# Moving one ternary weight piece within a sequence's fusion, and the FFN norm's layout to the last recurrence pass

## The chip, the cores and the metric

The kernel runs on one core of one Trainium2 chip. The metric is the device time of one execution in microseconds; the median of three runs before the change is 1723.41 us (1723.16 to 1723.78). All times in the trace are counted from the start of the profiled span.

## The reference

Eight sequences of 512 tokens and 512 channels go through a four-layer bidirectional gated recurrence, a fusion of both directions, and a feed-forward network with ternary weights. Both directions use the same recurrence weights. Cut to what matters:

```python
def _mingru(x, Wz, bz, Wh, bh):
    z = sigmoid(x @ Wz.T + bz)
    h_tilde = tanh(x @ Wh.T + bh)
    a = clip(1.0 - z, 1e-8, 1.0 - 1e-8)
    return linear_scan(a, z * h_tilde)
def _stack(x, ...):                     # forward, and on the flipped sequence
    for i in range(4):
        h_new = _mingru(h, ...)
        if i > 0:
            h_new = h_new + h
        h = layernorm(h_new, gamma, beta)
x = x + concat(h_fwd, h_bwd) @ fusion_W.T + fusion_b
# feed-forward
Wq = sign(W) * min(round(abs(W) / (mean(abs(W)) + 1e-6)), 1)
h = gelu(layernorm(x) @ Wq_fc.T)
h = layernorm(h) * ln_w + ln_b
x = x + h @ Wq_proj.T
```

## The kernel before

The channels lie on the 128 partitions in four chunks (`NC_` = 4), the tokens in four tiles (`NT` = 4). A sequence index is `b`; a recurrence stream is `s = (b, direction)`. The sequences are taken in pairs: (0, 1), (2, 3), (4, 5) and (6, 7). For each pair, layers 1 to 3 run over the streams (b,0), (b,1), (b+1,0), (b+1,1); then the two sequences are fused, tile by tile, with the first layer of the next pair put between the fusion tiles. The feed-forward network (FFN) runs after all eight sequences.

All the order is written out by hand. Each engine executes its instructions in the order in which the program issues them. One **slot** (`slot`, L407) issues a piece of main work on the tensor engine (PE), then the due turns and turns back of layer norms, then the scans, then the end of the main work.

- A **gates** slot (L422) does one output chunk of a layer: four matmuls by the program, eight in the trace, into a PSUM tile `u`; three activations on ScalarE (ACT: `a`, `t`, `z`, L444 to L446); on VectorE (DVE) a clip (L450), a product (L451) and a scan (L455). In the last layer the residual sums (L520) follow.
- A **turn** (L301) transposes one token tile into a PSUM tile `pt`. DVE takes its statistics (L156, L158, L162, L167), GpSimd (POOL) the inverse root (L163), ACT the normalised tile `tok` (L173, L174). There are two `pt` buffers (`ps_t`). A **turn back** (L310) transposes four `tok` tiles into `pf`, of which there are two buffers (`ps_f`).
- A **fusion tile** (`tile_of`, L536) adds the bias to a row tile on DVE (L542), takes a number of weight pieces (L543), does sixteen matmuls (L548) into two PSUM tiles, and at its end adds them to the row (L558) and stores it (L561).
- A **first-layer** chunk (L470) is scaled on DVE (L477) and scanned in both directions.

**Weight pieces.** The list `extra` holds small independent jobs; `pieces(n)` (L398) takes n of them and issues the loads of up to three pieces from the head of the list ahead. First come 32 pieces that sum absolute weights, then the thresholds; then 32 pieces that make the weights ternary (`quantised`, L599): two DVE operations (L178, L179) from a loaded tile (`fcb` or `pwb`, three buffers in `stgp`) into a tile `q` (two buffers in `qp`, named `fcq` and `pwq` in the trace), and a store to DRAM (L605) on SP's DMA queue. The tuple in L543 sets how many each fusion tile takes: four in the fusion of an even sequence, eight in that of an odd one. The four of sequence 0 are the end of the sums and thresholds; the ternary pieces run from sequence 1 to sequence 5, when they are used up.

**The norm's layout.** In the last pair, `combined()` (L616) adds four more jobs to `extra`: they spread the FFN norm's weight and bias over a tile `comb`, each as a rounded part (L623) and a remainder (L624). They are taken one after each gates slot of one stream's last layer (L524). `comb` is read first in the FFN, at L768. In the same passes the FFN's input of sequence 0 is turned: PE transposes into `py` (L199, in the `pf` buffers), ACT writes `yhi` (L204), DVE `ylo` (L205).

Of the kernel before, what the change touches and what calls it, by code (L numbers as in the profile page):

```python
# [24 lines left out]
def kernel(  # L25
# [27 lines left out]
    B, S, H = x.shape  # L53
    L = gru_wT.shape[0]
    F = fc_wT.shape[1]
    NC_ = H // P
    NT = S // P
# [61 lines left out]
    for i in range(2):  # L119
        s = const.tile([P, P], F32, name=f"fpick{i}")  # L120
# [88 lines left out]
    NW = NQ * NC_  # L209
# [4 lines left out]
    with rec:  # L214
# [58 lines left out]
        def need(*keys):  # L273

            while any(left.get(k) for k in keys):
                slot(None, 2)
# [48 lines left out]
        def norm(s, zs, tag, pause, pair=1):  # L325

            toks, at = Tokens(), now[0] + pause

            def dst():
                if s not in state:  # L330
                    state[s] = hp.tile([P, NC_, S], F32, tag="h", name=f"h_{s[0]}{s[1]}")
                return state[s]

            for t in range(NT):
                queue(turns, s, at, t // pair, tokens(turned(zs, t, f"{tag}_{t}", NC_), toks, None, f"{tag}_{t}"))
            for c in range(NC_):
                queue(backs, s, toks, c // pair, back(toks, dst, c, True, f"{tag}_{c}"))

        def norm_last(s, tag):
            rsv[s] = small.tile([P, NT], F32, tag="rsv", name=f"rsv_{tag}")  # L340
            zs = [state[s][:, c, :] for c in range(NC_)]
            for t in range(NT):
                queue(turns, s, now[0] + NC_ + 1, t, tokens(turned(zs, t, f"{tag}_{t}"), None, rsv[s][:, t : t + 1], f"{tag}_{t}"))
# [45 lines left out]
        extra = []  # L389
# [8 lines left out]
        def pieces(n):  # L398

            for _ in range(min(n, len(extra))):  # L400
                for piece in extra[:3]:
                    if piece[0] is not None:
                        piece[0]()
                        piece[0] = None
                extra.pop(0)[1]()

        def slot(work=None, cap=1, long=False):  # L407

            end = work() if work is not None else None
            due("factors")  # L410
            if long:
                due("scans")
            last = shares(cap) + x_shares()
            due("scans")
            if end is not None:
                end()
            due("resid")
            for f in last:
                f()
            now[0] += 1  # L420

        def gates(h, l, o, name, scans):  # L422

            def work():
                u = ps_u.tile([P, S], F32, tag="u", name=f"u_{name}")
                for c in range(NC_):
                    nc.tensor.matmul(  # L427
                        u, lhsT=gw[l][:, c, ts(o, P)], rhs=h[:, c, :],
                        start=(c == 0), stop=(c == NC_ - 1),
                    )  # L430
                z = zp.tile([P, S], F32, tag="z", name=f"z_{name}")
                zlive[0] += 1
                a, t = factors(u, z, l, o, name)

                def end():
                    product(a, z, t)
                    scans(a, z)
                return end
            return work
# [13 lines left out]
        def scan(dst, a, z, backward):  # L453
            d = slice(None, None, -1) if backward else slice(None)
            nc.vector.tensor_tensor_scan(dst[:, d], a[:, d], z[:, d], 0.0, ALU.mult, ALU.add)  # L455
# [47 lines left out]
        def layer(s, l):  # L503
            while s not in state:
                slot(None, 2)
            need(s)
            zs = []
            h = state[s]
            for o in range(NC_):
                def scans(a, z, o=o):  # L510
                    scan(z, a, z, s[1] == 1)
                    zs.append(z)
                    if l < L - 1:
                        nc.vector.tensor_tensor(z, z, h[:, o, :], ALU.add)  # L514
                    elif o == NC_ - 1:

                        for c in range(NC_):
                            def sums(c=c):
                                zlive[0] -= 1
                                nc.vector.tensor_tensor(h[:, c, :], zs[c], h[:, c, :], ALU.add)  # L520
                            stages.append((now[0] + c, "resid", sums))
                slot(gates(h, l, o, f"{s[0]}{s[1]}_{l}_{o}", scans))

                if s[0] < 2 and (l == L - 1 or o % 2) and len(extra) > 2 * NW or s == (B - 2, 1) and l == L - 1:  # L524
                    pieces(1)
            now[0] -= 1
            if l < L - 1:
                norm(s, zs, f"{s[0]}{s[1]}_{l}", 2)
            else:
                norm_last(s, f"{s[0]}{s[1]}_{l}")  # L530
            now[0] += 1

        def fusion(b):
            hs, rs = [], []

            def tile_of(t):  # L536
                def work():
                    if t == 0:
                        hs.extend(state.pop((b, d)) for d in range(2))
                        rs.extend(rsv.pop((b, d)) for d in range(2))  # L540
                    row = xs["f", b, t]
                    nc.vector.tensor_tensor(row, row, fb, ALU.add)  # L542
                    pieces((1, 2, 1, 0, 2, 2, 2, 2)[t + (b % 2) * NT])  # L543
                    pus = []
                    for d in range(2):
                        pu = ps_u.tile([P, H], F32, tag="u", name=f"pu_{b}_{t}_{d}")
                        for c in range(NC_):
                            nc.tensor.matmul(  # L548
                                pu, lhsT=hs[d][:, c, ts(t, P)], rhs=fw[:, d * NC_ + c, :],
                                start=(c == 0), stop=(c == NC_ - 1),  # L550
                            )
                        pus.append(pu)

                    def end():

                        assert all(left[b, d] < NT - t for d in range(2))
                        for d in range(2):
                            nc.vector.scalar_tensor_tensor(  # L558
                                row, pus[d], rs[d][:, t : t + 1], row, ALU.mult, ALU.add
                            )  # L560
                        nc.sync.dma_start(out=x1[b][t], in_=row)  # L561
                    return end
                return work
            return [tile_of(t) for t in range(NT)]
# [118 lines left out]
        for b in range(0, B, 2):  # L683
# [11 lines left out]
            for l in range(1, L):  # L695
                if last_pair:
                    load_fc(l - 1)
                    if l == 1:
                        combined()
                        load_pw(0)  # L700
                for s in ((b, 0), (b, 1), (b + 1, 0), (b + 1, 1)):
                    if l == L - 1 and not last_pair and s[1] == 0:
                        norm_x(s[0] + 2, now[0])
                    if l == L - 1 and s[1] == 0:
                        load_pair("f", s[0])
                    if l == L - 2 and not last_pair and s[1] == 1:
                        load_pair("n", s[0] + 2)
                        load_xT(s[0] + 2)
                    if last_pair and s == (b, 1) and l == L - 2:
                        load_y(0)  # L710
                    if last_pair and s == (b, 0) and l == L - 1:
                        norm_y(0)
                    layer(s, l)
                    if b == 0 and l == 1 and s[0] == 0:
                        fold_sums(s[1])
                    if b == 0 and l == 2:
                        if s[0] == 0:
                            fold(s[1])
                        elif s[1] == 0:
                            fold_bias()  # L720
# [34 lines left out]
    for i in range(2):  # L755
        s = const.tile([P, P], F32, name=f"pick{i}")
# [132 lines left out]
    for j in range(ends):  # L889
        b, k = divmod(j, NF)  # L890
# [81 lines left out]
```

## Time and profile before

| | |
|---|---|
| runs before, median of 3 | 1723.41 us (1723.16 to 1723.78) |
| profiled execution | 1722.93 us, its span 1720.9 us |
| granted PE clock | 0.999 |
| recurrence and fusion | 0 to about 1225 us |
| FFN | about 1225 us to the end |
| first fusion tile of an odd sequence starts at (PE, L548) | 321.18, 620.87, 919.90 us |
| last fusion tile of an odd sequence starts at (PE, L548) | 354.86, 654.56, 953.59 us |
| last layer of (6,1) on PE (L427) | 1117.35 to 1133.15 us |
| last layer of (7,1) on PE (L427) | 1151.93 to 1167.14 us |

The first column of a timeline line is the start in us, the second how long the group was busy; then engine, line, operation, tiles written and read, and the number of instructions; in brackets the idle time of the engine just before and what ended it. The ends of matmuls are modelled, so starts are compared with starts.

### The profile page before, as it was taken

The numbers are of one execution on the slowest core, as the hardware profiler recorded it, in microseconds if no ns is written. First come the engines' busy times: TensorE is split into PE (matmuls) and PEld (weight loads), VectorE is DVE, ScalarE is ACT, GpSimd is POOL, SyncE is SP. The second block draws the span as 40 slices with busy tenths as digits, with TensorE's granted clock in tenths as the row PEclk, the third lists the DMA queues.
The fourth block names the chain that finished last, engine by engine and source line by source line (L and its number), as shares of the span: only waits on it lengthen the run. The fifth ranks groups of instructions, "written<-read, shape, count | busy, mean of one in ns | idle before, by whom it ended". The sixth has DMA issues, their size and how long they took to land.

```text
span 1720.9 us, 19726 instructions
## 1 busy us (share of the span) xinstructions
PE 1703.8 (99%) x6424; PEld 1039.2 (60%) x6424; DVE 1452.0 (84%) x2865; ACT 1067.6 (62%) x1836; POOL 214.3 (12%) x334
## 2 busy tenths in 40 slices
PE   8999999999999999999999999999999999999998
PEld 4455554455555445555544555554688888888887
DVE  8989989889998998999899899995568778768876
ACT  4898883468886245888624688861266566566654
POOL 2111111111111111111111111110000000000000
PEclk9999999999999999999999999999999999999999
DMA  7002221250000115000012201202201101101100
GB/s 269 19 25 80 98 86 43 68 189 1 1 13 19 55 68 189 1 1 16 16 55 80 92 5 46 74 1 97 75 1 50 49 1 49 50 12 38 50 19 31
DMA packets 46454, 91.73 MB, mean 53 GB/s; under 512 B 5264, under 2 KB 5264, under 8 KB 45328
## 3 DMA queue, kind: packets, MB, share of 16 engines
q1 hardware_dynamic: 45488, 88.91, 15.0%
q10 hardware_dynamic: 864, 1.57, 0.3%
q8 instruction: 50, 0.82, 0.2%
q14 instruction: 52, 0.43, 0.1%
HBM read 65.30 MB, written 25.17 MB: 53 GB/s over the span
## 4 chain that ended last, share of the span: by engine, by line
PE 75%; DVE 19%; issue 4%; ACT 1%; POOL 0%; DMA 0%; DVEq 0%; POOLq 0%
PE u L427 29%; PE ph L789 12%; PE po L816 12%; PE pu L548 9%; PE pt L301 5%; DVE z L455 4%; PE pf L310 4%; PE u L470 3%; DVE st L156 3%; DVE z L451 2%; DVE zf L455 1%; DVE a L450 1%; DVE mv L158 1%; PE py L199 1%; DVE z L514 1%
## 5 line engine op out<-in xcount | busy, mean ns | idle before, releaser
L427 PE MATMUL u<-h,gw 128*128 128x512 f32 x768 | 345.5, 592 | 0.0
L427 PE MATMUL u<-xT,gw 128*128 128x512 f32 x768 | 345.4, 593 | 0.0
L455 DVE TENSOR_TENSOR_SCAN z<-a,z 128x512 f32<-128x512 f32 x224 | 274.2, 1224 | 7.6
L793 ACT ACTIVATE g<-ph 128x512 f32<-128x512 f32 x128 | 76.5, 597 | 240.5 <-PE ph L789 240.5
L427 PEld LDWEIGHTS u<-h,gw 128*128 128x128 f32 x768 | 138.7, 190 | 139.2 <-issue 138.7
L427 PEld LDWEIGHTS u<-xT,gw 128*128 128x128 f32 x768 | 138.7, 190 | 139.2 <-issue 138.0
L444 ACT ACTIVATE a<-u,ngb 128x512 f32<-128x512 f32 x192 | 131.7, 686 | 142.8 <-PE u L427 142.3
L156 DVE BATCH_NORM_STATS2 st<-pt 128x6 f32<-128x512 f32 x256 | 177.1, 692 | 49.7 <-PE pt L301 49.2
L163 POOL TENSOR_TENSOR rs<-ve,mhalf 128x1 f32<-128x1 f32 x192 | 123.0, 641 | 713.3 <-DVE nmu L167 658.3
L816 PE MATMUL po<-pwq,ghi 128*128 128x512 f32 x512 | 203.5, 397 | 0.0
L789 PE MATMUL ph<-yhi,fcq 128*128 128x512 f32 x512 | 199.7, 390 | 0.0
L816 PE MATMUL po<-pwq,glo 128*128 128x512 f32 x512 | 199.6, 390 | 0.0
L789 PE MATMUL ph<-ylo,fcq 128*128 128x512 f32 x512 | 199.4, 389 | 0.0
L451 DVE TENSOR_TENSOR z<-z,t 128x512 f32<-128x512 f32 x224 | 153.4, 685 | 8.5 <-ACT z L446 8.3
L174 ACT ACTIVATE tok<-pt,nmr,rs 128x512 f32<-128x512 f32 x192 | 149.3, 778 | 6.4
L804 DVE TENSOR_TENSOR acc<-acc,g 128x512 f32<-128x512 f32 x112 | 77.3, 690 | 87.9 <-ACT g L793 87.0
L446 ACT ACTIVATE z<-u,gb 128x512 f32<-128x512 f32 x192 | 132.4, 689 | 0.0
L445 ACT ACTIVATE t<-u,gb 128x512 f32<-128x512 f32 x192 | 130.8, 681 | 0.0
L301 PEld LDWEIGHTS pt<-ident,z 128*128 128x128 f32 x640 | 78.4, 141 | 82.4 <-issue 47.5
L548 PE MATMUL pu<-fw,xT 128*128 128x512 f32 x256 | 115.2, 593 | 0.0
L548 PE MATMUL pu<-fw,h 128*128 128x512 f32 x256 | 115.1, 592 | 0.0
L470 PE MATMUL u<-xT,gw 128*128 128x512 f32 x256 | 114.6, 593 | 0.3 <-DVE gw L673 0.3
(138 smaller groups left out, 2549.5 us busy)
## 6 DMA issues: line engine op xcount, KB each, us to landing
xn<-in_x_dram SPq DMA_DIRECT2D x32, 256.0 KB, 4.4
xf<-in_x_dram SPq DMA_DIRECT2D x32, 256.0 KB, 5.6
x<-xf SPq DMA_DIRECT2D x32, 256.0 KB, 2.0
xy<-x SPq DMA_DIRECT2D x32, 256.0 KB, 4.5
out_dram<-xy SPq DMA_DIRECT2D x32, 256.0 KB, 2.0
xT<-in_xt_dram SPq DMA_DIRECT2D x7, 1024.0 KB, 8.1
fca<-in_fc_wT_dram SPq DMA_DIRECT2D x16, 256.0 KB, 2.9
pwa<-in_proj_wT_dram SPq DMA_DIRECT2D x16, 256.0 KB, 2.6
```

Of the source, the lines that this page charges most:

```text
L156: nc.vector.bn_stats(st, src)
L174: nc.scalar.activation(dst, src, AF.Identity, bias=nmr, scale=rs)
L301: nc.tensor.transpose(pt[:, ts(c, P)], zs[c][:, ts(t, P)], ident)
L427: nc.tensor.matmul(u, lhsT=gw[l][:, c, ts(o, P)], rhs=h[:, c, :], start=(c == 0), stop=(c == NC_ - 1),)
L444: nc.scalar.activation(a, u, AF.Sigmoid, bias=ngb[:, l, o : o + 1], scale=-1.0)
L446: nc.scalar.activation(z, u, AF.Sigmoid, bias=gb[:, l, o : o + 1])
L451: nc.vector.tensor_tensor(z, z, t, ALU.mult)
L455: nc.vector.tensor_tensor_scan(dst[:, d], a[:, d], z[:, d], 0.0, ALU.mult, ALU.add)
L470: nc.tensor.matmul(u, lhsT=gw[0][:, c, ts(o, P)], rhs=xT[b][:, c, :], start=(c == 0), stop=(c == NC_ - 1),)
L548: nc.tensor.matmul(pu, lhsT=hs[d][:, c, ts(t, P)], rhs=fw[:, d * NC_ + c, :], start=(c == 0), stop=(c == NC_ - 1),)
L789: nc.tensor.matmul(ph, lhsT=w, rhs=ys[b][c][i], start=(c == 0 and i == 0), stop=(c == NC_ - 1 and i == 1),)
L816: nc.tensor.matmul(po[b][t], lhsT=part[:, ts(t, P)], rhs=pwq[k // NP_][:, k % NP_, :], start=(k == 0 and i == 0), stop=(k == NF - 1 and i ...
```

## The change

Two lines. The tuple in the fusion says how many pieces each tile takes: the first four numbers are for an even sequence, the last four for an odd one. For an odd sequence 2, 2, 2, 2 becomes 1, 2, 2, 3. The condition in `layer` now takes the four jobs of the norm's layout in the last layer of stream (7,1) instead of (6,1).

```diff
-                if s[0] < 2 and (l == L - 1 or o % 2) and len(extra) > 2 * NW or s == (B - 2, 1) and l == L - 1:
+                if s[0] < 2 and (l == L - 1 or o % 2) and len(extra) > 2 * NW or s == (B - 1, 1) and l == L - 1:
                     pieces(1)
...
-                    pieces((1, 2, 1, 0, 2, 2, 2, 2)[t + (b % 2) * NT])
+                    pieces((1, 2, 1, 0, 1, 2, 2, 3)[t + (b % 2) * NT])
```

Sequence 7 is odd too, but no piece is left when its fusion runs. In sequences 1, 3 and 5 the fifth to eighth number decide. The pieces keep their order; one piece of work in each of the three moves from the first tile to the last, after which the next pair's layer 1 begins.

## The prediction

> **What bounds the kernel now.** I read the page first (busy shares, the chain that ended last), then PE's waits, the windows by stage, and the timelines of PE, DVE, ACT and SP around the edited places.
>
> ```profile
> PE 1703.8 (99%) x6424; PEld 1039.2 (60%) x6424; DVE 1452.0 (84%) x2865; ACT 1067.6 (62%) x1836; POOL 214.3 (12%) x334
> ...
> PE 75%; DVE 19%; issue 4%; ACT 1%; POOL 0%; DMA 0%; DVEq 0%; POOLq 0%
> ...
> PE pt L301 <- ACT tok L174: 4.4, 11, 0.6
> ...
> 310.00:334.60 24.60, 24.07 (x79) 11.83 (x78) 23.51 (x47) 10.12 (x18) 3.15 (x5) 1.00 0.19 60
> 334.60:363.00 28.40, 28.40 (x98) 14.81 (x97) 22.02 (x40) 11.36 (x19) 2.05 (x3) 1.00 0.43 133
> ```
>
> PE is never idle for long; a change pays only where it closes a PE gap. The chain runs 19% through DVE, but most of that is DVE keeping pace. In the windows (length, then PE, PEld, DVE, ACT, POOL busy), 310 to 334.6 has DVE at 23.51 of 24.60 us while PE loses 0.5; the next has PE full and DVE with 6.4 us to spare. The gap between the two, on PE and on DVE:
>
> ```profile
> 328.92 3.60 PE L470 MATMUL u<-xT,gw 128*128 128x512 f32 x8
> 332.56 0.66 PE L301 MATMUL pt<-ident,z 128*128 128x128 f32 x4
> 333.70 0.66 PE L301 MATMUL pt<-ident,z 128*128 128x128 f32 x4 [0.49 <-ACT tok L174]
> 334.20 0.60 PE L310 MATMUL pf<-ident,tok 128*128 128x128 f32 x4
> 334.63 3.60 PE L548 MATMUL pu<-fw,xT 128*128 128x512 f32 x8
> ...
> 323.70 0.48 DVE L178 TENSOR_SCALAR fcq<-fcb,lo_fc 128x512 f32<-128x512 f32 x1
> 324.22 0.75 DVE L179 SCALAR_TENSOR_TENSOR fcq<-fcb,hi_fc,fcq 128x512 f32<-128x512 f32 x1
> 324.88 0.48 DVE L178 TENSOR_SCALAR fcq<-fcb,lo_fc 128x512 f32<-128x512 f32 x1
> ...
> 329.53 0.67 DVE L156 BATCH_NORM_STATS2 st<-pt 128x6 f32<-128x512 f32 x1
> ...
> 362.37 0.70 DVE L156 BATCH_NORM_STATS2 st<-pt 128x6 f32<-128x512 f32 x1 [4.34 <-PE pt L301]
> ```
>
> A chunk of eight matmuls holds PE 3.44 us start to start, four transposes 0.44. From 328.92 the two turns (L301), the turn back (L310) and the fusion matmuls could start at 332.36, 332.80, 333.23 and 333.67; the fusion starts at 334.63, so 0.96 us is lost. It is lost on DVE: the turns wait for a PSUM buffer that ACT's tok empties, tok waits for the statistics, and they stand behind the two weight pieces at 323.70 and 324.88. The stage recurs 298 us apart (PE turns at 633.40 and 932.43, equally late).
>
> The last pair has its own gap:
>
> ```profile
> 1132.99 0.60 PE L310 MATMUL pf<-ident,tok 128*128 128x128 f32 x4
> 1134.20 0.66 PE L199 MATMUL py<-ident,tok_y 128*128 128x128 f32 x4 [0.61 <-DVE ylo L205]
> ...
> 1130.08 0.68 DVE L624 TENSOR_TENSOR comb<-lnw,comb 128x512 fp32r<-128x512 f32 x1
> 1131.02 0.68 DVE L451 TENSOR_TENSOR z<-z,t 128x512 f32<-128x512 f32 x1
> 1133.46 0.68 DVE L205 TENSOR_TENSOR ylo<-py,yhi 128x512 fp32r<-128x512 f32 x1
> ...
> 1174.92 0.70 DVE L156 BATCH_NORM_STATS2 st<-pt 128x6 f32<-128x512 f32 x1 [2.73 <-PE pt L301]
> ```
>
> py is due at 1133.43 and starts at 1134.20: 0.77 lost, behind ylo, which stands behind two of the comb operations. Another 0.15 is lost at 1128.97.
>
> **What the Trainium skill says.** "Perfetto Trace Analysis", Optimization Strategy: look for the gaps of the engine that should be saturated and what they wait for; the trace bears it out, those gaps are the only place where this change can pay. "PSUM — Partial Sum Buffer", Engine vs sequencer instructions: VectorE's queue is strictly first in, first out, so whatever is behind a held ternary waits too; DVE's timeline keeps program order. "VectorE: DVE Perf Modes", TRN2 errata, gives 691 ns for a two-tensor f32 operation of 512 elements; L451 measures 685. "DMA: Bandwidth & Descriptors", Latency and other measured facts, has about 2 us of fixed cost per DMA; the stores of pieces (L605) land here 2.0 to 4.3 us after issue.
>
> **The change, part by part.** No instruction is added or removed overall: 32 weight pieces and four comb operations stay.
>
> *First tile of sequences 1, 3, 5: one piece fewer.* On SP a load and a store move later too. On DVE the pitch of a piece is 324.88 - 323.70 = 1.18 us. DVE has been without idle time since 309.55, so what follows moves up by 1.18 until something else holds it. That is the statistics at 329.53: they would reach 328.35, but read the turn that PE starts at 328.05, and statistics begin 0.64 after their turn (361.73 to 362.37, 366.48 to 367.12). So 328.69, a gain of 0.84. The second set, released afresh, follows 1.15 later (362.37 to 363.52), at 329.84 instead of 330.65: 0.81. POOL's and ACT's steps follow alike, tok from 332.87 to 332.06, and the second turn, 0.83 behind tok, from 333.70 to 332.89, where PE arrives at 332.80. Gain 0.81 of the 0.96. The other two stages have the same pitches (629.23 against a turn at 627.74; 928.25 against 926.77): 3 x 0.81 = 2.43 us. Does the wait come back? DVE later idles 0.92 before the scaling at 346.45, held by PE, so it catches up. The 0.39 that PE loses at 375.49 hangs on a chain restarted by PE at 366.48; it stays. So do the gaps before the edited tile (0.15 at 320.68, 0.59 at 620.38, 0.24 at 919.41).
>
> *Last tile: one piece more.* 1.18 us into 4.34 us of DVE idle before 362.37 (4.35 in the other two). The third ternary has a wait that the second has not: there are two q buffers (qp), so it needs the store of the tile's first piece landed. That store is issued at 356.87 and lands 3.14 later, 360.01; 0.81 earlier in the new order, 359.2. The third piece then ends at about 360.5, before the statistics' new 361.56: 1.1 us to spare. Its own load (issued 355.46, landed 359.31) comes sooner. For sequence 3 the store lands at 659.96, leaving 0.8 us; for sequence 5 at 957.61, over 2 us. Cost 0. Behind the waiting ternary stand the statistics of two turns and the x1 sums; an overrun would first use the 1.1 us by which tok (364.60, done 365.38) precedes PE's turn at 366.48. Bounds: 0 while the store lands within 5.3 us, one for one beyond (rival 3).
>
> *Comb operations out of sequence 6.* Ahead of ylo at 1133.46 go 0.34 (cast at 1125.52) and 0.60 (L624). Not all 0.94 counts: L451 at 1131.02 needs ACT's z, and follows z's start by 0.72 (1134.35 to 1135.07). ACT's three activations start 3.64 after PE's chunk (1129.55 to 1133.19); for the chunk at 1125.10 that is 1128.74 instead of 1128.80, so z starts at 1129.88 and L451 at 1130.60: gain 0.42. ylo and py follow, py 1133.78. Bounds: 0.3 (a 0.21 issue gap as at 1127.30 moving in front) to 0.92.
>
> *Comb operations into sequence 7's last pass.* DVE there runs at 3.87 us per slot (statistics at 1156.02, 1159.89, 1163.76), exactly PE's 3.44 + 0.43, without slack; so delays of 0.34, 0.94, 1.27 and 1.87 pile up. PE asks little of DVE there: a turn needs the buffer of two turns before, nearly 7 us earlier, and its h sums were finished by 1152.2, before the first added operation. The pile ends with the row addition at 1171.51, done at 1172.19 + 1.87 = 1174.06, before the 2.73 us idle ends at 1174.92. Cost 0; up to 1.87 without that cover. The comb's readers (L768) are in the FFN.
>
> **Sum:** -2.43 - 0.42 = -2.85 us. The profiled execution took 1722.93 (span 1720.9 and 2.0 around it), 0.48 below the median; the difference applies to either. 1723.41 - 2.85 = 1720.6.
>
> **The rivals.** A difference of 0.2% (3.45 us), about what can be told from no change, is the line between classes.
> (1) All of the gaps close: 3 x 0.96 + 0.77 + 0.15 = 3.80 us, 1719.6. For it: DVE and ACT have 0.2 us issue gaps near these places (335.23, 1127.30) that may move away. Against: the 0.64 behind the turn is measured twice, alike.
> (2) The gain is mostly taken back, say half: 1722.0, or 1723.4 if all. It would show as a new tok wait after 334.6. Against: DVE's 0.92 and 6.4 us of slack there.
> (3) Slower: the store wait. If, with its loads around it, the first store of the last tile took 7.5 us to land, the third piece would start at 363.5 and end at 364.8, 3.2 past 361.56; less the 1.1 before PE's turn, 2.1 per stage, 6.4 in three, and 6.4 - 2.85 = +3.6: 1727.0. A landing of 5.3 us begins to cost (3.14 + 1.1 + 1.1), and from 6.3 on the gain is gone. For it: a load took 1.57 us to issue at 655.15. Against: no piece store took over 4.3 us.
> That a piece simply doesn't move is excluded by the count: each odd sequence still takes eight, and four comb items remain for the last pass.
>
> **How the numbers follow.** Forecast (gain 2.2 to 3.45) 0.62; rival 1, 0.20; rival 2, 0.10; rival 3, 0.08. Faster by over 0.2%: 0.22 (rival 1 and the forecast's edge); within: 0.70; slower: 0.08. The range 1719.5 to 1722.3 holds the forecast, nearly all of rival 1 and half of rival 2.
>
> **What would show it.** Right: PE's fusion matmuls of the first odd tile 0.8 us sooner in three stages, the tok wait before them gone or 0.1; DVE idle in the last tile down from 4.34 to 1 to 2 us with the statistics still released by PE; py's wait on ylo near 0.35 instead of 0.77; DVE's 2.73 idle near 1174 down to about 0.9. Wrong: a third ternary waiting past 361, a PE wait between 1152 and 1175, or a tok wait that reappears after 334.6.

## The result and the profile after

The changed kernel takes 1720.88 us (median of 22 runs, 1720.01 to 1721.71), the kernel before 1723.59 (22 runs beside it): a ratio of 0.9984, 95% interval 0.9978 to 0.9990. The difference of 2.71 us is 0.16%, inside the 0.2% that the prediction takes as the line to no change, although the interval leaves out 1. The profiled span went from 1720.9 to 1718.0 us.

Because the profiled executions differ by up to 1.8 us before the first odd fusion tile (the turn ahead of its fusion matmuls starts between 320.57 and 322.33 us in the profiles below), the traces are compared over a **stretch**: from that turn to the second matmul of the FFN (PE, L789). It was 1226.09 - 320.68 = 905.41 us before and is 1223.19 - 320.57 = 902.62 after, 2.79 less.

From the page of the kernel after, the busy shares and the chain that ended last:

```profile
PE 1702.4 (99%) x6424; PEld 1039.2 (60%) x6424; DVE 1452.8 (85%) x2865; ACT 1067.8 (62%) x1836; POOL 214.6 (12%) x334
...
PE 79%; DVE 14%; issue 4%; ACT 1%; DMA 1%; POOL 0%; DVEq 0%; POOLq 0%; ACTq 0%
```

The work is the same. In the chain DVE's part fell from 19 to 14% and PE's rose from 75 to 79%. This says that DVE sets the pace less often, but not how much was gained: 5% of the span is 86 us, and the gain is 2.8. The waits and the windows show that. PE's waits after (total us, times, longest), then its windows around the first odd tile (length; PE, PEld, DVE, ACT and POOL busy; clock, DMA share, GB/s):

```profile
PE pt L301 <- ACT tok L174: 2.9, 8, 0.6
...
PE py L199 <- DVE ylo L205: 0.4, 1, 0.4
```

```profile
310.00:334.60 24.60, 24.60 (x82) 12.36 (x81) 23.13 (x48) 10.88 (x19) 3.39 (x6) 1.00 0.15 47
334.60:363.00 28.40, 28.40 (x98) 14.81 (x97) 23.26 (x43) 11.29 (x18) 2.04 (x4) 1.00 0.45 145
```

Three of the eleven listed waits for tok are gone, 1.5 us, and PE is full in the first window. DVE's 1.2 us went over to the second, from 22.02 to 23.26; the first falls by 0.38 only, since later work moves up into it. The first odd tile on PE's timeline after, and on DVE's:

```profile
328.81 3.60 PE L470 MATMUL u<-xT,gw 128*128 128x512 f32 x8
332.24 1.19 PE L301 MATMUL pt<-ident,z 128*128 128x128 f32 x8
333.27 0.60 PE L310 MATMUL pf<-ident,tok 128*128 128x128 f32 x4
```

```profile
324.10 0.75 DVE L179 SCALAR_TENSOR_TENSOR fcq<-fcb,hi_fc,fcq 128x512 f32<-128x512 f32 x1
324.77 0.42 DVE L450 TENSOR_SCALAR a<-a 128x512 f32<-128x512 f32 x1
...
328.57 0.70 DVE L156 BATCH_NORM_STATS2 st<-pt 128x6 f32<-128x512 f32 x1 [0.26 <-PE pt L301]
```

The clip L450 now follows one weight piece. The statistics are released by their turn (327.93, so 0.64 after it), no longer by DVE's queue, and the two turns on PE stand in one group. From its start to the turn back 1.03 us pass, where two turns without a wait take 0.87: about 0.15 of the 0.96 is left, as forecast. The fusion matmuls follow at 333.71 instead of 334.63: of this 0.92, 0.11 is the earlier chunk (328.81 against 328.92), 0.81 the gain.

The last tile on DVE's timeline after:

```profile
356.35 0.75 DVE L179 SCALAR_TENSOR_TENSOR fcq<-fcb,hi_fc,fcq 128x512 f32<-128x512 f32 x1
358.95 0.48 DVE L178 TENSOR_SCALAR fcq<-fcb,lo_fc 128x512 f32<-128x512 f32 x1 [1.85 <-DMA wq_fc<-fcq]
359.47 0.75 DVE L179 SCALAR_TENSOR_TENSOR fcq<-fcb,hi_fc,fcq 128x512 f32<-128x512 f32 x1
361.44 0.70 DVE L156 BATCH_NORM_STATS2 st<-pt 128x6 f32<-128x512 f32 x1 [1.23 <-PE pt L301]
```

The third piece waits 1.85 us for the store of the first (`wq_fc<-fcq`), ends 1.2 us ahead of the statistics, and PE still releases those. Of 4.34 us of idle time, 1.85 + 1.23 are left. The same place in sequence 3 is the closest of the three:

```profile
658.56 0.49 DVE L178 TENSOR_SCALAR pwq<-pwb,lo_pw 128x512 f32<-128x512 f32 x1 [2.55 <-DMA wq_pw<-pwq]
...
660.36 0.70 DVE L156 BATCH_NORM_STATS2 st<-pt 128x6 f32<-128x512 f32 x1 [0.53 <-PE pt L301]
```

There 0.53 us are to spare, and in sequence 5 1.88.

The last pair, on PE's and on DVE's timeline after:

```profile
1130.34 0.60 PE L310 MATMUL pf<-ident,tok 128*128 128x128 f32 x4
1131.30 0.66 PE L199 MATMUL py<-ident,tok_y 128*128 128x128 f32 x4 [0.36 <-DVE ylo L205]
```

```profile
1128.11 0.69 DVE L451 TENSOR_TENSOR z<-z,t 128x512 f32<-128x512 f32 x1 [0.73 <-ACT z L446]
...
1130.56 0.68 DVE L205 TENSOR_TENSOR ylo<-py,yhi 128x512 fp32r<-128x512 f32 x1
...
1172.02 0.70 DVE L156 BATCH_NORM_STATS2 st<-pt 128x6 f32<-128x512 f32 x1 [0.90 <-PE pt L301]
```

L451 is no longer behind comb operations but waits for ACT's z; ylo follows two operations later. py starts 0.96 after the turn back, so 0.52 late instead of 0.77 (the 0.36 in brackets is the counterpart of the 0.61 before), and the loss of 0.15 one slot earlier is gone. The comb operations, now in the last pass of (7,1), leave 0.90 of the 2.73 us of idle time.

### The profile page after: what moved, and what is told of

The parts are those of the page before. It is cut to its first block, busy times and chain, and to the rows that moved or that the text cites. A ratio compares the mean times of both kernels' runs of the same rounds, so it can differ in the third digit from the quotient of the medians.

```text
span 1718.0 us, 19725 instructions
## 1 busy us (share of the span) xinstructions
PE 1702.4 (99%) x6424; PEld 1039.2 (60%) x6424; DVE 1452.8 (85%) x2865; ACT 1067.8 (62%) x1836; POOL 214.6 (12%) x334
## 3 DMA queue, kind: packets, MB, share of 16 engines
q10 hardware_dynamic: 864, 1.57, 0.3%
## 4 chain that ended last, share of the span: by engine, by line
PE 79%; DVE 14%; issue 4%; ACT 1%; DMA 1%; POOL 0%; DVEq 0%; POOLq 0%; ACTq 0%
PE u L427 30%; PE ph L789 12%; PE po L816 12%; PE pu L548 11%; PE pt L301 5%; PE pf L310 4%; PE u L470 4%; DVE z L455 4%; DVE st L156 2%; DVE z L451 2%; DVE zf L455 1%; DVE a L450 1%; PE py L199 1%; DVE z L514 1%; DVE mv L158 1%
## 5 line engine op out<-in xcount | busy, mean ns | idle before, releaser
L789 PE MATMUL ph<-yhi,fcq 128*128 128x512 f32 x512 | 199.7, 390 | 0.0
L789 PE MATMUL ph<-ylo,fcq 128*128 128x512 f32 x512 | 199.4, 389 | 0.0
L451 DVE TENSOR_TENSOR z<-z,t 128x512 f32<-128x512 f32 x224 | 153.4, 685 | 9.7 <-ACT z L446 9.5
```

The source lines that it names most:

```text
L451: nc.vector.tensor_tensor(z, z, t, ALU.mult)
L789: nc.tensor.matmul(ph, lhsT=w, rhs=ys[b][c][i], start=(c == 0 and i == 0), stop=(c == NC_ - 1 and i == 1),)
```

## The experiments

My theory: the gain is that of two separate DVE queues (three first tiles, one last pass), set by counts of operations, and the moved work costs nothing because idle time covers it. The rivals: the tile's gain comes from something else, the layout is what pays, or the cover was nearly used up. Medians are in us; the stretch is from one profile each.

| run | median (runs) | before beside it | ratio, 95% interval | stretch |
|---|---|---|---|---|
| the change | 1720.88 (22) | 1723.59 | 0.9984 (0.9978 to 0.9990) | 902.62 |
| e1_tuple_only | 1721.49 (21) | 1723.61 | 0.9986 (0.9980 to 0.9993) | 903.05 |
| e2_layout_only | 1723.71 (13) | 1723.61 | 0.9999 (0.9991 to 1.0008) | 905.09 |
| e3_three_first | 1737.62 (4) | 1723.61 | 1.0081 (1.0068 to 1.0095) | 918.90 |
| e4_three_first_q3 | 1726.52 (15) | 1723.61 | 1.0018 (1.0010 to 1.0026) | 909.82 |
| e5_after_q3 | 1720.22 (20) | 1723.46 | 0.9981 (0.9975 to 0.9988) | 902.02 |
| e6_zero_first | 1723.54 (12) | 1723.46 | 1.0000 (0.9992 to 1.0008) | 905.53 |
| e7_five_last | 1727.88 (10) | 1723.46 | 1.0024 (1.0015 to 1.0033) | 909.44 |
| e8_even_too | 1720.70 (20) | 1723.46 | 0.9983 (0.9977 to 0.9990) | 903.33 |
| e9_layout_twice | 1720.54 (15) | 1723.42 | 0.9983 (0.9976 to 0.9991) | 902.57 |
| e10_third_tile | 1720.06 (13) | 1723.42 | 0.9979 (0.9971 to 0.9988) | 901.98 |

**Each part alone.** Against the changed kernel:

```diff
# e1_tuple_only
-                if s[0] < 2 and (l == L - 1 or o % 2) and len(extra) > 2 * NW or s == (B - 1, 1) and l == L - 1:
+                if s[0] < 2 and (l == L - 1 or o % 2) and len(extra) > 2 * NW or s == (B - 2, 1) and l == L - 1:
# e2_layout_only
-                    pieces((1, 2, 1, 0, 1, 2, 2, 3)[t + (b % 2) * NT])
+                    pieces((1, 2, 1, 0, 2, 2, 2, 2)[t + (b % 2) * NT])
```

> Only the tuple changes (1, 2, 2, 3); the norm's layout stays in sequence 6. My theory: the three stages give 3 x 0.81 = 2.43 us, so about 2.4 us below before, and 0.4 us above the full change; py still starts 0.77 late behind ylo. Rival (the two edits share one gain, or the layout does most of it): less than 1.5 us below before.

> Only the norm's layout moves to sequence 7; the tuple stays 2, 2, 2, 2. My theory: 0.42 us below before, since after the two operations are gone ylo waits for ACT's z and py remains 0.5 late; the four operations in sequence 7 cost nothing, DVE's idle time before the statistics near 1174 falls from 2.7 to about 0.9 us. Rival A (all 0.94 us of the removed DVE time counts): 0.9 below. Rival B (DVE without slack in sequence 7 passes its 1.87 us on to PE): 1 to 1.5 us above before.

With the tuple alone the stretch is 2.36 shorter than before, with py still 0.78 late. With the layout alone it is 0.32 shorter, the turns of the first odd tile as late as before, and py of the last pair as after the change:

```profile
1133.92 0.60 PE L310 MATMUL pf<-ident,tok 128*128 128x128 f32 x4
1134.88 0.66 PE L199 MATMUL py<-ident,tok_y 128*128 128x128 f32 x4 [0.36 <-DVE ylo L205]
```

The parts add up: 2.36 + 0.32 = 2.68, against 2.79 together. The times say less: the tuple's effect stands, the layout's lies inside its interval and is shown by the trace alone.

**More pieces in the first tile.** If DVE's queue sets the first tile's end, pieces added there must cost what the sum says. Both runs start from the kernel before, so the layout stays in (6,1), and take 3, 2, 2, 1 in the odd sequence; e4 also has a third buffer for q, a tile that no one uses at that time:

```diff
# e3_three_first and e4_three_first_q3, against the kernel before
-                    pieces((1, 2, 1, 0, 2, 2, 2, 2)[t + (b % 2) * NT])
+                    pieces((1, 2, 1, 0, 3, 2, 2, 1)[t + (b % 2) * NT])
# e4_three_first_q3 (also e5, e8, e10), in quantised
-                q = qp.tile([P, 512], F32, tag="q", name=f"{name}q_{i}")
+                turn[0] += 1
+                if turn[0] % 3:
+                    q = qp.tile([P, 512], F32, tag="q", name=f"{name}q_{i}")
+                else:
+                    q = both.rearrange("p c i r -> p (c i r)")
```

> The edit turned round: the first tile of an odd sequence takes three pieces and the last one (3, 2, 2, 1), layout as before, two q buffers. The third piece of the first tile must then wait for the store of the first, where nothing covers it: store issued 325.0, landed 327.6 in the trace of before, against DVE free at 326.07. My theory: 1.6 us of wait and 1.18 us of work reach PE, about 2.8 us in each of three stages, 8 us above before. Rival (the chain through DVE only keeps pace with PE, a piece more costs nothing): as before.

> As the run with three pieces in the first tile, but every third piece writes its ternary weights into a tile that is free by then, so there are three q buffers in turn and the third piece need not wait for the first one's store. My theory: only the work counts, 1.18 us in each of three stages, about 3.5 us above before; PE's second turn waits 1.2 us longer than before. Rival (it is the store, or the DMA traffic, not DVE's time that holds the stage): as with two buffers, 8 us above.

At the turns e4 behaves as the sum says: the first turn is 1.39 late in each of the three stages, instead of 0.20, one pitch of a piece (1.18) more, 3.5 us in all. PE's timeline of e4:

```profile
333.74 0.66 PE L301 MATMUL pt<-ident,z 128*128 128x128 f32 x4 [1.23 <-ACT tok L174]
334.88 0.66 PE L301 MATMUL pt<-ident,z 128*128 128x128 f32 x4 [0.49 <-ACT tok L174]
```

The time is 2.9 us above before, and that it comes near 3.5 is in part chance. In the trace three other gaps (near 530, 623 and 1139 us) are together 0.9 us shorter than before, and one stage loses 1.7 us more to a lower clock, as told below. In e3 the third ternary waits 1.57 us besides, for the store of the first, and the turn is 3.05, 3.16 and 2.95 late, as computed. But e3 costs 14.0 us, where 8 had been expected. PE's timeline of e3 and two windows of it:

```profile
329.79 3.60 PE L470 MATMUL u<-xT,gw 128*128 128x512 f32 x8
336.27 0.66 PE L301 MATMUL pt<-ident,z 128*128 128x128 f32 x4 [2.88 <-ACT tok L174]
337.42 0.93 PE L301 MATMUL pt<-ident,z 128*128 128x128 f32 x4 [0.49 <-ACT tok L174]
338.14 1.06 PE L310 MATMUL pf<-ident,tok 128*128 128x128 f32 x4
338.99 4.64 PE L548 MATMUL pu<-fw,xT 128*128 128x512 f32 x8
343.46 2.74 PE L548 MATMUL pu<-fw,h 128*128 128x512 f32 x6
```

```profile
336.20:338.50 2.30, 1.74 (x10) 1.50 (x11) 2.19 (x5) 1.93 (x5) 0.02 (x1) 0.82 0.30 108
338.50:341.40 2.90, 2.90 (x8) 1.59 (x7) 2.66 (x9) 2.83 (x6) 1.50 (x2) 0.56 0.44 98
```

After the wait the granted clock falls to about a half: the turn back takes 0.85 start to start instead of 0.44, the first fusion chunk 4.47 instead of 3.44. With a part of the second turn's group this is 1.6 to 1.7 us in each stage, 4.9 in all. The late turns make 8.5, and the stretch is 13.5 longer than before. The Trainium skill ("TensorE: Matmul & The Clock Gate", HAM oscillation — how this bites in real kernels) says that the clock is taken back where PE has idle gaps of over some 3.4 us. Here 2.88 us, then four transposes and 0.49 more, were enough in all three stages. In e4's profile, 1.23 us followed by 0.49 was enough in one stage of three (clock 0.52 between 336.0 and 339.3). So shorter waits than the page's were followed by it here, but no run shows from which length on. The 0.49 alone, in the kernel before, was not (clock 1.00 from 334.6).

**The cover under the last tile.** If the last tile had room for more than one piece, taking the first tile's last piece there, or one from each other tile, should show how much:

```diff
-                    pieces((1, 2, 1, 0, 1, 2, 2, 3)[t + (b % 2) * NT])
# e6_zero_first
+                    pieces((1, 2, 1, 0, 0, 2, 2, 4)[t + (b % 2) * NT])
# e7_five_last
+                    pieces((1, 2, 1, 0, 1, 1, 1, 5)[t + (b % 2) * NT])
```

> Tuple 0, 2, 2, 4 for an odd sequence, layout in sequence 7, two q buffers. My theory: the first tile gives nothing more, because after one piece less its statistics already wait for PE's turn (0.26 us of DVE idle, which grows to about 1.4); the fourth piece in the last tile waits for the second one's store and ends about where the statistics are due. So as the full change, within 0.5 us. Rival (every piece taken out of the first tile pays): 2.4 us or more below the full change.

> Tuple 1, 1, 1, 5 for an odd sequence, layout in sequence 7, two q buffers: the cover of the last tile is overdrawn. Each piece from the third on waits for the store of the one two before; I put the fifth piece's end near 364.7 where the statistics are due at 361.4, 3.3 us late. My theory: 1.1 us of that is covered by ACT's lead on PE, and about 2 us in each of three stages reaches PE: 5 to 7 us above the full change. Rival (the last tile has room for any number): as the full change.

In e6 the first tile gives nothing more, as expected, since there the statistics are bound by their turn already. But the run is at the time of before, 2.7 above the change, against an expected difference of under 0.5. DVE's timeline of e6 in the last tile, and the two turns on PE's timeline that follow:

```profile
361.83 0.48 DVE L178 TENSOR_SCALAR fcq<-fcb,lo_fc 128x512 f32<-128x512 f32 x1 [2.97 <-DMA wq_fc<-fcq]
...
363.71 0.49 DVE L178 TENSOR_SCALAR fcq<-fcb,lo_fc 128x512 f32<-128x512 f32 x1 [0.61 <-DMA wq_fc<-fcq]
364.24 0.75 DVE L179 SCALAR_TENSOR_TENSOR fcq<-fcb,hi_fc,fcq 128x512 f32<-128x512 f32 x1
364.91 0.69 DVE L156 BATCH_NORM_STATS2 st<-pt 128x6 f32<-128x512 f32 x1
```

```profile
367.96 0.66 PE L301 MATMUL pt<-ident,zf 128*128 128x128 f32 x4 [0.49 <-ACT tok L174]
...
376.46 0.66 PE L301 MATMUL pt<-ident,z 128*128 128x128 f32 x4
377.72 0.66 PE L301 MATMUL pt<-ident,z 128*128 128x128 f32 x4 [0.60 <-ACT tok L174]
```

The fourth piece, and the wait for stores with two q buffers, put the statistics at 364.91. Their turn was at 362.57, so 363.21 was due: 1.70 late. PE's turn is 0.65 late for it, so 1.05 us were free. Then two later turns are 0.26 and 0.76 late, where after the change the second alone was late, by 0.39: another 0.63. Sequence 3 loses about as much in the trace (0.76, 0.27 and 0.75 late), sequence 5 nothing. In e7 the same: statistics 2.47 late (364.68, turn 361.57), the turn at 367.73 1.41 late, again 1.06 free, and the same 0.63 at 376 to 377. In the other two stages that turn is 1.87 and 1.30 late, with the same 0.63 behind it. e7 comes to 7.0 us above the change in the median, at the upper end of what was expected.

**Better versions.** A third q buffer takes away the wait for stores. e5 adds nothing else to the change; e8 also moves a piece from the even sequences' third tile to the odd ones' last; e10 puts that piece in the odd ones' third tile. All use e4's buffer:

```diff
-                    pieces((1, 2, 1, 0, 1, 2, 2, 3)[t + (b % 2) * NT])
# e8_even_too
+                    pieces((1, 2, 0, 0, 1, 2, 2, 4)[t + (b % 2) * NT])
# e10_third_tile
+                    pieces((1, 2, 0, 0, 1, 2, 3, 3)[t + (b % 2) * NT])
```

> The full change with a third q buffer (a tile that is free by then). The third piece of the last tile no longer waits for the first one's store, but still for its own load. My theory: DVE's wait in the last tile shortens by half a microsecond or more, and the time stays that of the full change within noise, since PE's turn at the tile's end releases the statistics anyway. Rival (the store wait reaches PE): up to 1 us below the full change.

> A version meant to beat the change: the third tile of an even sequence gives up its piece too (1, 2, 0, 0), the last tile of an odd one takes four (1, 2, 2, 4), with three q buffers. The remaining PE waits before the odd sequence's first tile (0.58 at 619.5, 0.27 at 917.7, 0.16 at 320.6) hang on DVE work that stands behind that piece. My theory: 0.8 us below the full change, those waits down to 0.1. Rival (the fourth piece in the last tile overdraws the cover): 1 us above the full change.

In e5 the third piece waits 1.14 us for its own load instead of 1.85 for a store, and the statistics keep 1.93 us to spare. That pays nothing there; the stretch is 0.60 shorter because two other gaps shrank (526.86 us from 0.48 to 0.18, 619.77 from 0.58 to 0.26; the last section has more on them). In e8 the gaps that it aimed at fell (619.57 us to 0.16, 918.57 from 0.27 to 0.16). Of the first, 0.32 is gone in e5 too, so the moved pieces close only 0.10 and 0.11. In the last tile the loads came too late. DVE's timeline of e8:

```profile
358.73 0.49 DVE L178 TENSOR_SCALAR fcq<-fcb,lo_fc 128x512 f32<-128x512 f32 x1 [1.26 <-DMA fcb<-in_fc_wT_dram]
...
361.40 0.49 DVE L178 TENSOR_SCALAR fcq<-fcb,lo_fc 128x512 f32<-128x512 f32 x1 [1.40 <-DMA fcb<-in_fc_wT_dram]
361.92 0.75 DVE L179 SCALAR_TENSOR_TENSOR fcq<-fcb,hi_fc,fcq 128x512 f32<-128x512 f32 x1
362.59 0.69 DVE L156 BATCH_NORM_STATS2 st<-pt 128x6 f32<-128x512 f32 x1
...
368.50 0.69 DVE L451 TENSOR_TENSOR z<-z,t 128x512 f32<-128x512 f32 x1 [0.38 <-ACT z L446]
```

The statistics are 0.78 late (turn at 361.17), less than the 1.05 that were free at the next turn, and that turn is on time. Yet the late tok puts ACT's next three activations 0.5 late, L451 then waits 0.38 for ACT's z, a wait that the changed kernel does not have, and the turn at 375.39 is 0.76 late instead of 0.39. In sequence 3 turns are 0.12, 0.26 and 0.76 late. So the expected 0.8 us did not come. In e8 and e10 the stretch also holds two small matmuls of the thresholds (L590), since sequence 0 gives up a job too: they run at 321.2 us in e8, behind the first turn, and near 294 after the change. They add 0.22 us to the stretch. e10 was made from what e8 showed:

> Even sequences take (1, 2, 0, 0) and odd ones (1, 2, 3, 3), with the third q buffer: against the run with (1, 2, 2, 4) one piece goes from the last tile to the third tile of the odd sequences. My theory: the gaps before the first odd tile stay closed as in that run (619.6 and 918.6 near 0.16 instead of 0.58 and 0.27, 526 near 0.16), and the last tile, now with three pieces, has its statistics released by PE again, so the turns at 375 and 674 stay at 0.39: about 1.0 us below the changed kernel, near 1719.8, the lowest of all versions. The third tile has on VectorE 1.10 us of idle before the scaling at 346.43 but none from there to 356; so the added 1.18 us delays its scans, and the last tile's own pieces, by 1.18 us, and what idle time is left before the statistics at 362.4 (1.9 plus 1.1 us) takes it up. Rival: the delayed scans are what the last tile's turns wait for, and PE loses up to 1.2 us per stage there: 3.5 us longer, near 1723.5.

DVE's timeline of e10 in the last tile, and its turn on PE's timeline:

```profile
360.38 0.49 DVE L178 TENSOR_SCALAR fcq<-fcb,lo_fc 128x512 f32<-128x512 f32 x1 [0.90 <-DMA fcb<-in_fc_wT_dram]
360.91 0.75 DVE L179 SCALAR_TENSOR_TENSOR fcq<-fcb,hi_fc,fcq 128x512 f32<-128x512 f32 x1
362.65 0.70 DVE L156 BATCH_NORM_STATS2 st<-pt 128x6 f32<-128x512 f32 x1 [1.00 <-PE pt L301]
```

```profile
375.78 0.66 PE L301 MATMUL pt<-ident,z 128*128 128x128 f32 x4 [0.23 <-ACT tok L174]
```

PE releases the statistics again, the turn is back at 0.39, and the gaps at 527, 620 and 918 us are 0.15 to 0.16. The stretch, 901.98, is the shortest, 0.64 below the change (1.0 had been expected), and so is the median. Without the 0.22 of the thresholds it would be 0.86 below the change and 0.26 below e5. It is faster than before; from the changed kernel and from e5 the medians don't tell it apart.

**The layout's cover.** The four comb operations issued twice:

```diff
# e9_layout_twice
+                    again = extra[0][1] if s == (B - 1, 1) else None
                     pieces(1)
+                    if again is not None:
+                        again()
```

> The changed kernel, with each of the four comb operations issued twice in the last pass of stream (7,1), so that VectorE carries twice the added work there (the result is the same; the second issue of an operation repeats the first). The pile of delays on VectorE grows from 1.87 to 3.74 us, 0.97 more than the 0.90 us of idle time left before the statistics at 1172.02, which would then start near 1173.0. My theory (nothing on PE asks for VectorE's results between 1152 and 1175, and the 2.77 us idle before 1179.77 absorbs the rest): no PE gap appears there, time within 0.3 us of the changed kernel's over the stretch. Rival (the 0.90 us were the last cover, so the layout in the last pass was close to its limit): PE loses about 1.0 us between 1172 and 1190, and the time is 1.0 us longer. Second rival (the scans lag so far behind that a turn of the last pass waits): a PE gap already before 1172.

DVE's timeline of e9:

```profile
1173.31 0.68 DVE L545 TENSOR_TENSOR xf<-xf,fb 128x512 f32<-128x512 f32 x1
1173.91 0.69 DVE L156 BATCH_NORM_STATS2 st<-pt 128x6 f32<-128x512 f32 x1
...
1180.26 0.70 DVE L156 BATCH_NORM_STATS2 st<-pt 128x6 f32<-128x512 f32 x1 [1.39 <-PE pt L301]
```

The pile overruns the 0.90 us: the statistics no longer wait for PE. But PE has no gap there, the idle time before the next statistics falls from 2.77 to 1.39, and the stretch is 902.57. The cover under the layout is deeper than the 0.90 us that the trace shows in front of one instruction.

## Why the prediction was right

The forecast was 1720.6 us, 2.85 below before; measured are 1720.88 and 2.71.

- **First odd tile, one piece fewer:** predicted 0.81 in each stage, 2.43 in all, bound by the statistics 0.64 behind their turn. The trace shows 0.81 in the first stage; e1 gives 2.36 for the three, and e6 shows that a second piece taken away gives nothing more. Right in mechanism and size.
- **Last tile, one piece more:** predicted a third ternary that waits for a store, ends near 360.5 and costs nothing, with 1.1 us to spare. It ended at 360.2 with 1.23 to spare; in sequences 3 and 5 0.53 and 1.88 are left, where 0.8 and over 2 were forecast. The fallback, never used, that an overrun is free for 1.1 us was half right: the next turn has 1.05 us of lead (e6, e7), but a delay of 0.78 already costs 0.4 later, at the second turn after it (e8). The price of rival 3, which rested on it, was too low for that reason.
- **Comb operations out of (6,1):** predicted 0.42, bound by ACT's z. L451 does wait for z; PE gained 0.92 - 0.52 = 0.40 at its gaps, and e2's stretch is 0.32 shorter. The medians are too coarse for a term of this size. The term had been worked out at py alone (0.35 late). In the trace it is 0.25 at py and 0.15 one slot earlier: as PE comes to py 0.15 sooner, py is still 0.52 late. The sum is the same.
- **Comb operations into (7,1):** predicted cost 0, idle time down to about 0.9. It is 0.90, and even twice the work costs nothing (e9).
- **Not touched:** the gaps near 320.6, 374.6, 526, 619.5 and 917.7 are as before (0.16, 0.40, 0.48, 0.58 and 0.27). That 374.6 hangs on a chain restarted by PE holds only as long as DVE is on time, as e6 to e8 show.

Of the rivals, (1) is excluded by py's 0.52 and (2) by PE's full window after 334.6. Rival 3's mechanism exists, as e6 shows, but took a fourth piece: with three, the statistics kept 0.53 us or more to spare in every stage. The smallest, in sequence 3, was nearer to costing than the first stage alone shows.

## What to carry to other kernels

Where an in-order engine serves the bound engine, a piece of filler work is worth moving only until the next releaser takes over: count the operations between the filler and the late instruction, and find the next wait that holds that instruction. The gain is the smaller of two times: that of the work taken away (1.18 us here), or that until the next wait takes over (0.81). For the place that takes the work, look at what its own data and buffers wait for (here stores and loads of 2 to 5 us, not the 1.18 us of operations), and follow a delay past the first turn, since it can reach PE one or two turns later through another engine's queue. Test a cover by doubling the work under it.

## What the runs showed of the hardware

In two runs waits of PE were followed by a time at about half the clock, and so cost more than their length. In e3, waits of 2.88 and 0.49 us were followed by about 3.4 us in which a matmul took 0.85 us start to start instead of 0.43, in all three stages; in e4 waits of 1.23 and 0.49 did this once (335.8 to 339.2 us) and twice not. What decides between these was not tried.

DVE also has stalls that no wait explains. DVE's timeline of the kernel after:

```profile
515.90 0.43 DVE L450 TENSOR_SCALAR a<-a 128x512 f32<-128x512 f32 x1 [0.25 <-issue]
...
578.15 1.60 DVE L558 SCALAR_TENSOR_TENSOR xf<-pu,rsv,xf 128x512 f32<-128x512 f32 x2 [0.23 <-issue]
```

Behind the first PE has its gap near 526 us, behind the second the one near 619.5. All eight kernels with two q buffers have both stalls (0.23 to 0.25 us), whatever their tuple; the four with a third one (e4, e5, e8, e10) have neither. In these four the gap near 526 is 0.15 to 0.18 instead of 0.44 to 0.48, and the one near 619.5 is 0.16 to 0.26 instead of 0.57 to 0.60. Set beside the change's timeline, e5's DVE gains 0.33 us at the first place and 0.31 at the second, about what the two gaps shrank by. So e5's 0.60 us goes with the third buffer, not with the order of the pieces. In the changed kernel no piece runs between 361 and 575 us, so the first stall is not a wait for a q buffer. Whether the place of the instructions in the program sets it stays open: no run moves them and leaves the buffers alone.
